# Expert results scattered to rows of the tokens, in place of a gather per choice, in a GNN and mixture-of-experts kernel

## The chip, the cores and the metric

The kernel runs on one core of a Trainium2 chip. The time is that of the device, in microseconds (us), for one execution. The engines are TensorE (PE, matmuls), VectorE (DVE), ScalarE (ACT), GpSimd (POOL) and SyncE (SP), which here only starts DMA transfers. An indirect DMA takes a list of row numbers, one for each of the 128 partitions, and moves each partition's row from such a row of a table (a gather) or to it (a scatter); in this kernel POOL issues all of them.

## The reference

Two blocks with residual connections, on 3125 nodes of 256 channels. The first is a graph attention layer over 50,000 edges; the change does not touch it. The second is a mixture of eight experts, of which each token uses the two with the largest router weights:

```python
x = x + gnn(layernorm(x), edges)
tokens = layernorm(x)
probs = softmax(tokens @ router_w.T)                # 3125 x 8
rw, re = top_k(probs, 2);  rw = rw / rw.sum(-1)     # two experts and their weights
combine = zeros(3125, 8);  combine[token, re] = rw
out = tokens
for e in range(8):
    y = gelu(tokens @ w1[e] + b1[e]) @ w2[e] + b2[e]    # 256 -> 256 -> 256
    out = out + combine[:, e:e + 1] * y
x = x + out
```

## The kernel before

The nodes are cut into 25 tiles of 128 tokens (the last has 53), one token to a partition. The graph part fills the first 790 us. Then comes the part that the change touches. It is written by hand in the order that PE, DVE, ACT and SP are to follow; POOL's order is left to the scheduler, which follows the data.

**Front.** POOL gathers the graph layer's result rows (`fetch_rows`, L1337: one gather for each token tile, 21 first and four later) into `tok_all`, 128 x 25 x 256. DVE adds a tile to `xs` (the running x) and takes its mean and variance (`add_stats`, L1377); ACT and DVE turn these into a scale (`root`, `scale`), ACT writes the normalised tokens over `tok_all` (`tokens`, L1409), PE transposes them and multiplies them with the router. The token tiles form three parts of 8, 10 and 7 (`PARTS`). For each part a `Route` finds the two experts of each token (`exps`, L1441, and on), and `places` (L1447) works out where the token goes: the (token, choice) pairs of a part are put in order of their expert, each expert's share padded to full tiles of 128 rows. `place[q]` holds the row number of a token's choice q. POOL then scatters each token row twice, by these numbers, to the table `xd` in DRAM (L1514; 16, 20 and 14 scatters). The parts make 23, 27 and 20 expert tiles, 70 in all. What of the routing isn't needed at once (the expert of each tile, the gates, part 2's places) runs as small steps inside the main loop, two to a tile.

**Main loop** (L1714), one round for each expert tile n:

- SP loads the tile n + 4 of `xd` (`load`, L1632) to `xt`.
- `turn(n + 1)` (L1647): DVE copies the expert's first weights (`w1_t`), ACT its second ones (`w2_t`), PE transposes `xt`, and DVE copies the result out (`xT`).
- `up(n)` (L1659): four matmuls, and gelu with the bias on ACT (`gT`).
- `down(n - 1)` (L1671): two matmuls, DVE copies the result to `ys`, and SP stores `ys` as 128 whole rows of the table `yd`, at the same place as the tile had in `xd`.
- ACT adds the layernormed tokens to `xs` in every second round (`with_input`).
- Two rounds after a part's last tile has been stored, POOL begins to gather its results: for each token tile and each choice one gather of 128 rows of `yd` by `place[q]` (`fetch_y`, L1685), with up to eight in flight; three rounds later DVE begins to add one of them each round, times its gate, to `xs` (`add_y`, L1692). Parts 0 and 1 make 36 gathers, of which 31 are added in the loop.

**Tail.** After the last expert tile DVE makes the adds that are left. The second bias, `combine @ b2`, is a matmul of eight rows for each token tile (`second_bias`, L1696), for which PE transposes `comb` (the gates by expert) four token tiles at a time. This runs for the 18 token tiles of parts 0 and 1, each with its store to the output (`store`, L1702); then for each of the 7 tiles of part 2 come two gathers, the bias, two adds and the store.

Of the kernel before, what the change touches and what calls it, by code (L numbers as in the profile page):

```python
# [17 lines left out]
P = 128  # L18
N = 3125
C = 256  # L20
# [40 lines left out]
def expert_tiles(a, b):  # L61

    pairs = 2 * (min(b * P, N) - a * P)
    return (pairs + EXP * (P - 1)) // P

# [326 lines left out]
def gnn_ffn_kernel(ctx: ExitStack, tc: tile.TileContext, x, src, dst, W, att_src, att_dst, bias,  # L392
# [162 lines left out]
    zrow = late.tile([P, C], F32, name="zrow")  # L555
    xd = [dram.tile([expert_tiles(a, b) * P, C], F32, name=f"xd{i}") for i, (a, b) in enumerate(PARTS)]
    yd = [dram.tile([expert_tiles(a, b) * P, C], F32, name=f"yd{i}") for i, (a, b) in enumerate(PARTS)]

    def load_late():
        for x in range(4):  # L560
            nc.sync.dma_start(b2_sb[32 * x:32 * x + EXP, :], b2)
        nc.sync.dma_start(b1_sb, b1)
        nc.sync.dma_start(rw_in, router_w)
        for i, (a, b) in enumerate(PARTS):
            nc.sync.dma_start(xd[i].rearrange("(t p) c -> p t c", p=P),
                              zrow[:, None, :].to_broadcast([P, expert_tiles(a, b), C]))
# [116 lines left out]
    G.memset(zrow, 0.0)  # L683
    nc.sync.dma_start(res[NONE:, :], bias_b[:NRES - NONE, :])
# [651 lines left out]
    tok_all = fin.tile([P, NT, C], F32, name="tok_all")  # L1336
    def fetch_rows(a, b):  # L1337
        for t in range(a, b):
            G.indirect_dma_start(out=tok_all[:, t, :], out_offset=None, in_=res,
                                 in_offset=bass.IndirectOffsetOnAxis(ap=res_row[:, t:t + 1], axis=0))  # L1340
# [15 lines left out]

    desc = fin.tile([P, EXP], F32, name="desc")
# [19 lines left out]
    def add_stats(a, b):  # L1377
        for t in range(a, b):
            V.tensor_add(xs[:, t, :], xs[:, t, :], tok_all[:, t, :])  # L1379
            V.bn_stats(st[:, t, :], xs[:, t, :])  # L1380
            V.bn_aggr(mv[:, t, :], st[:, t, :])
# [27 lines left out]
    def tokens(a, b):  # L1409

        for t in range(a, b):
            S.activation(tok_all[:, t, :], xs[:, t, :], AF.Identity, bias=c0[:, t:t + 1], scale=rs[:, t:t + 1])  # L1412
            p = psF.tile([P, 2, P], F32, name="tp")
            for kc in range(2):
                T.transpose(p[:, kc, :], tok_all[:, t, kc * P:(kc + 1) * P], ident)  # L1415
            copy_out()
            turned.append((t, p))
        if any(b == e for _, e in PARTS):
            copy_out()
            router()  # L1420
# [5 lines left out]
    class Route:  # L1426
# [20 lines left out]
        def places(self):  # L1447
# [57 lines left out]
            for q in range(2):  # L1505
                V.tensor_mul(tmp, at, oh[q])
                yield
                V.tensor_reduce(rowf, tmp, axis=AX.X, op=ALU.add)
                yield
                V.tensor_copy(place[q][:, a:b], rowf)  # L1510
# [121 lines left out]
    def load(n):  # L1632
        if n < len(tiles):
            i, j = tiles[n]
            xt[n] = fin2.tile([P, C], F32, name="xt", bufs=n_load + 2)
            nc.sync.dma_start(xt[n], xd[i][j * P:(j + 1) * P, :])
# [34 lines left out]
    def down(n):  # L1671
        if n >= 0:
# [4 lines left out]
            ys = fin2.tile([P, C], F32, name="ys", bufs=4)  # L1677
            V.tensor_copy(ys, py)  # L1678
            nc.sync.dma_start(yd[i][j * P:(j + 1) * P, :], ys)
# [5 lines left out]
    def fetch_y(i, t, q):  # L1685
        m = rows_at(t)
        y = fin2.tile([P, C], F32, name="y", bufs=8)
        G.indirect_dma_start(out=y[:m], out_offset=None, in_=yd[i],  # L1688
                             in_offset=bass.IndirectOffsetOnAxis(ap=place[q][:m, t:t + 1], axis=0))
        return t, q, y  # L1690

    def add_y(t, q, y):  # L1692
        m = rows_at(t)
        V.scalar_tensor_tensor(xs[:m, t, :], y[:m], gate[q][:m, t:t + 1], xs[:m, t, :], op0=ALU.mult, op1=ALU.add)  # L1694
# [7 lines left out]
    def store(t):  # L1702
        m = rows_at(t)
        m0 = m // 16 * 16
        nc.sync.dma_start(out[t * P:t * P + m0, :], xs[:m0, t, :])
        if m0 < m:
            nc.sync.dma_start(out[t * P + m0:t * P + m, :], xs[m0:m, t, :])

    steps = later()
    todo, fetched = {}, []  # L1710
# [3 lines left out]
    for n in range(len(tiles) + 1):  # L1714
# [5 lines left out]
        if n in ends[:-1]:  # L1720
            todo = [(i - 1, t, q) for t in range(*PARTS[i - 1]) for q in range(2)]
# [7 lines left out]
        if i and n > ends[i - 1] + 1:  # L1729
            while todo and len(fetched) < 8:  # L1730
                fetched.append(fetch_y(*todo.pop(0)))
            if n > ends[i - 1] + 4 and fetched:
                add_y(*fetched.pop(0))
    assert next(steps, 0) == 0 and not todo
    while fetched:
        add_y(*fetched.pop(0))
    cT = []
    for x in range(COMB):
        pt = psF.tile([P, P], F32, name="tp")
        T.transpose(pt, comb[:, 4 * x:4 * x + 4, :].rearrange("p t e -> p (t e)"), ident)  # L1740
        cT.append(fin.tile([P, P], F32, name=f"cT{x}"))
        S.copy(cT[x], pt)
    a, b = PARTS[-1]
    for t in range(a):
        second_bias(t)
        store(t)
    for t in (NT - 1, *range(a, NT - 1)):
        y = [fetch_y(len(PARTS) - 1, t, q) for q in range(2)]
        second_bias(t)
        for v in y:  # L1750
            add_y(*v)
        store(t)
# [29 lines left out]
```

## Time and profile before

| | us |
|---|---|
| median of 9 runs (1102.0 to 1110.7) | 1106.52 |
| the profiled execution | 1104.51 |
| its span, first to last instruction | 1102.7 |
| graph part, to | 790 |
| front: first statistics on DVE | 796.95 |
| first routing step of part 0 | 831.54 |
| main loop, first to last tile's result, about | 886 to 1075 |
| tail, last tile's copy to the end | 1074.7 to 1102.7 |

Granted clock of TensorE over the span: 0.84. Busy over the span: PE 807.0 us (73%), DVE 591.2 (54%), POOL 586.8 (53%), ACT 354.4 (32%). POOL's indirect DMAs of the changed part are 50 scatters to `xd` (50.6 us, 1013 ns each) and 50 gathers from `yd` (49.7 us, 993 ns each).

In the lines of the profile, L12 is line 12 of the kernel file, `a<-b` means that tile a is written from b, and "128x256 f32" is partitions by elements. The windows view gives the busy time and, in brackets, the number of instructions of each engine in a stretch of time; then the clock that TensorE was granted (1.00 is full speed), the share of time in which the DMA engines were busy, and the GB/s that they moved. The timeline lists instructions with their start, duration, engine and line, and the idle time of the engine before them, with the instruction or transfer that ended it; "remote" is a signal whose sender the profile could not name, and "issue" is time in which nothing that the profile shows was waited for.

### The profile page before, as it was taken

Reading aid. Unit: us, or ns where it says so; the run is one execution under the profiler, and the core shown is the slowest. Engines: PE = TensorE matmul, PEld = TensorE weight load, DVE = VectorE, ACT = ScalarE, POOL = GpSimd, SP = SyncE. Lnnn points to the kernel's source line nnn. Section 1 sums busy time; section 2 is a strip of 40 time slices with the busy share of each in tenths; the row PEclk is TensorE's granted clock in tenths of the full one; section 3 lists DMA queues with packets and bytes.
Section 4 is the critical chain, followed back from the end, with each engine's and each line's share of the span. In section 5 each row is a group of like instructions: output and inputs, shape, how many; then the busy total and the mean of one; then the engine's idle time right before and its main releaser. Section 6 shows DMA issues by size and latency. Waiting matters only on the chain. (4 is left out here: it accounts for less than half of the span.)

```text
span 1102.7 us, 14972 instructions
## 1 busy us (share of the span) xinstructions
PE 807.0 (73%) x4312; PEld 706.5 (64%) x4312; DVE 591.2 (54%) x1565; ACT 354.4 (32%) x1175; POOL 586.8 (53%) x606
## 2 busy tenths in 40 slices
PE   4842478787788787788887886899525559689794
PEld 3621377677677777677777775777324548579783
DVE  5753466557565565533444442587537315457476
ACT  3200233333333333333333332321124425356450
POOL 3857566566666666665666666304473350541335
PEclk9755689989999899989999898798855569899895
DMA  6354397444444444444444442109131223445456
GB/s 218 110 150 111 95 310 251 113 113 123 122 113 112 111 116 114 112 124 119 116 113 114 113 117 83 32 15 338 55 102 50 72 97 109 135 148 158 144 159 187
DMA packets 93883, 140.41 MB, mean 127 GB/s; under 512 B 17910, under 2 KB 72172, under 8 KB 93430
## 3 DMA queue, kind: packets, MB, share of 16 engines
q0 software_dynamic: 26640, 71.16, 24.4%
q1 hardware_dynamic: 61290, 65.48, 18.0%
q10 hardware_dynamic: 5856, 2.67, 0.9%
q8 instruction: 38, 0.62, 0.2%
q14 instruction: 59, 0.48, 0.1%
HBM read 102.74 MB, written 36.49 MB: 126 GB/s over the span
## 5 line engine op out<-in xcount | busy, mean ns | idle before, releaser
L930 POOL DMA_INDIRECT g<-xn_tab,srcS x392 | 378.0, 964 | 234.0 <-issue 92.2
L1020 PE MATMUL pz<-sel,g 128*128 128x176 f32 x1568 | 325.1, 336 | 12.4 <-issue 6.5
L1020 PEld LDWEIGHTS pz<-sel,g 128*128 128x128 f32 x1568 | 287.0, 208 | 38.7 <-issue 10.5
L1028 PE MATMUL pw<-W_sb,zs 128*128 128x256 f32 x800 | 258.9, 414 | 71.1 <-ACT zs L1022 64.4
L1022 ACT COPY zs<-pz 128x320 f32 x392 | 170.0, 434 | 409.9 <-PE pz L1020 240.7
L1028 PEld LDWEIGHTS pw<-W_sb,zs 128*128 128x128 f32 x800 | 149.4, 208 | 80.1 <-ACT zs L1022 73.3
L1514 POOL DMA_INDIRECT xd<-tok_all,place x50 | 50.6, 1013 | 88.0 <-issue 68.4
L1688 POOL DMA_INDIRECT y<-yd,place x50 | 49.7, 993 | 83.2 <-DMA yd<-ys 38.4
L1006 DVE TENSOR_TENSOR sel<-is_s,pa 128x704 f32<-128x704 f32 x100 | 82.0, 882 | 19.1 <-remote 8.6
L1665 PE MATMUL ph<-xT,w_t 128*128 128x128 f32 x560 | 79.2, 287 | 14.2 <-DVE xT L1657 11.4
L1676 PE MATMUL py<-w_t,gT 128*128 128x256 f32 x280 | 76.8, 400 | 17.2 <-issue 16.4
L1665 PEld LDWEIGHTS ph<-xT,w_t 128*128 128x128 f32 x560 | 71.7, 200 | 17.4 <-DVE xT L1657 13.9
L978 DVE COPY A<-pt 128x128 f32<-128x128 f32 x25 | 7.3, 292 | 129.1 <-PE pt L970 89.2
L1669 ACT ACTIVATE gT<-ph,bias_t 128x128 f32<-128x128 f32 x140 | 43.9, 364 | 96.6 <-PE ph L1665 57.6
L1023 ACT COPY zb<-pz 128x32 f32<-128x32 f32 x392 | 74.8, 191 | 0.2 <-DMA dr<-drel_d 0.2
L1678 DVE COPY ys<-py 128x256 f32<-128x256 f32 x70 | 29.7, 424 | 69.8 <-PE py L1676 45.1
L1676 PEld LDWEIGHTS py<-w_t,gT 128*128 128x128 f32 x280 | 50.5, 201 | 22.8 <-issue 17.4
L1041 DVE TENSOR_TENSOR ow<-pw,bias_b 128x256 f32<-128x256 f32 x22 | 9.3, 425 | 87.5 <-remote 77.0
L1415 PE MATMUL tp<-ident,tok_all 128*128 128x128 f32 x50 | 16.4, 443 | 49.2 <-ACT tok_all L1412 24.6
L999 PE MATMUL pa<-ident,A 128*128 128x128 f32 x25 | 8.5, 342 | 56.6 <-issue 23.4
L999 PEld LDWEIGHTS pa<-ident,A 128*128 128x128 f32 x25 | 3.5, 142 | 66.4 <-issue 31.5
L1652 ACT COPY w_t<-wb 128x512 f32 x70 | 43.0, 616 | 2.5 <-issue 1.7
(342 smaller groups left out, 1100.9 us busy)
## 6 DMA issues: line engine op xcount, KB each, us to landing
xt<-xd SPq DMA_DIRECT2D x70, 128.0 KB
yd<-ys SPq DMA_DIRECT2D x70, 128.0 KB
fl<-flag_d SPq DMA_DIRECT2D x50, 128.0 KB
dr<-drel_d SPq DMA_DIRECT2D x50, 128.0 KB
g<-xn_tab,srcS POOLq DMA_INDIRECT x392
xd<-zrow SPq DMA_DIRECT2D x1, 3456.0 KB
xs<-in_x_dram SPq DMA_DIRECT2D x4, 768.0 KB
out_dram<-xs SPq DMA_DIRECT2D x24, 128.0 KB
```

Of the source, the lines that this page charges most:

```text
L930: G.indirect_dma_start(out=g[-1][:, i % Q, :], out_offset=None, in_=xn_tab, in_offset=bass.IndirectOffsetOnAxis(ap=srcS[:, c:c + 1], axis=0))
L1006: V.tensor_tensor(t, is_s[:, i0:i1, None, :].to_broadcast([P, Q, H, SLOT]), pa[:, i0:i1, :, None].to_broadcast([P, Q, H, SLOT]), op=ALU.mult)
L1020: T.matmul(pz[:, kc].rearrange("p h s -> p (h s)"), g[i // Q][:, i % Q, kc * P:(kc + 1) * P], sel[i // Q][:, i % Q].rearrange("p h s -> p ...
L1022: S.copy(z[:, :, :, bass.ds(off, IC)], pz[:, :, :, :IC])
L1023: S.copy(zb[:, :, :, chunk(b, i), :].rearrange("p k h s -> p (k h) s"), pz[:, :, :, IC:].rearrange("p k h s -> p (k h) s"))
L1028: T.matmul(pw, z[:, kc, h, :P], W_sb[:, kc, h * C:(h + 1) * C], start=(i == 0 and not biased), stop=(i == CPS - 1))
L1514: ins = G.indirect_dma_start(out=xd[self.i], out_offset=bass.IndirectOffsetOnAxis(ap=place[q][:m, t:t + 1], axis=0), in_=tok_all[:m, t, :] ...
L1652: S.copy(w2_t[n], wb[:, bass.ds(expert_of(n, ACT_), 1), :])
L1665: T.matmul(ph[:, f, :], w1_t[n][:, 0, kc * C + f * P:kc * C + (f + 1) * P], xT[n][:, kc, :], start=(kc == 0), stop=(kc == 1))
L1669: S.activation(gT[n][:, f, :], ph[:, f, :], AF.Gelu, bias=routes[i].bias_t[:, f, j:j + 1])
L1676: T.matmul(py, gT[n][:, f, :], w2_t[n][:, 0, f * C:(f + 1) * C], start=(f == 0), stop=(f == 1))
L1688: G.indirect_dma_start(out=y[:m], out_offset=None, in_=yd[i], in_offset=bass.IndirectOffsetOnAxis(ap=place[q][:m, t:t + 1], axis=0))
```

## The change

The rows of `xd`, and with them `tok_all` and `xt`, become two numbers longer (`CY` = 258). The first extra column of a token's row holds the row of its first choice in `xd`, the second the address of a place of its own: each part's table `yd` gets, behind the `ROWS` rows for padding, two rows for each token. Since a token's row is scattered to both of its places, the row that an expert tile loads tells where its result is to go: if the row's own position equals the first extra number, the result is the first choice's and goes to the token's base row + 1, else to the base row; a padding row has -1 in both columns and keeps its own position. `down` works that out in two small DVE operations and POOL scatters `ys` by it, where SP stored it. Both results of a token then lie side by side, and SP loads them for a token tile with a plain DMA (`load_y`), where POOL gathered each choice.

The order of work changes too. The row numbers (`own_row`, `to_i`) are made by POOL and copied by DVE after the gathers of `fetch_rows` in the text, ahead of the first statistics. The results of part 0 are loaded and added in tiles 29 to 39, and then the second bias is added and the token tile stored in the same round; those of part 1 are loaded and added at tiles 56 to 68. In the tail the biases of the last 7 token tiles come before their loads, and those of part 1's ten come with stores on ACT's queue while the loads run. `xt` has seven buffers for six, `ys` twelve for four, `y` four for eight.

```diff
+CY = C + 2
+MOST = max(b - a for a, b in PARTS)
+ROWS = expert_tiles(0, MOST) * P
...
-    zrow = late.tile([P, C], F32, name="zrow")
-    xd = [dram.tile([expert_tiles(a, b) * P, C], F32, name=f"xd{i}") for i, (a, b) in enumerate(PARTS)]
-    yd = [dram.tile([expert_tiles(a, b) * P, C], F32, name=f"yd{i}") for i, (a, b) in enumerate(PARTS)]
+    zrow = late.tile([P, CY], F32, name="zrow")
+    xd = [dram.tile([expert_tiles(a, b) * P, CY], F32, name=f"xd{i}") for i, (a, b) in enumerate(PARTS)]
+    yd = [dram.tile([ROWS + 2 * MOST * P, C], F32, name=f"yd{i}") for i in range(len(PARTS))]
...
     G.memset(zrow, 0.0)
+    G.memset(zrow[:, C:], -1.0)
...
-    tok_all = fin.tile([P, NT, C], F32, name="tok_all")
+    tok_all = fin.tile([P, NT, CY], F32, name="tok_all")
...
+    own_row = fin.tile([P, 32], F32, name="own_row")
+    own_row_i = fin.tile([P, 32], I32, name="own_row_i")
+    G.iota(own_row_i, pattern=[[P, 32]], base=0, channel_multiplier=1)
+    to_i = fin.tile([P, NT, 1], I32, name="to_i")
+    for a, b in PARTS:
+        G.iota(to_i[:, a:b, 0], pattern=[[2 * P, b - a]], base=ROWS, channel_multiplier=2)
+    V.tensor_copy(own_row, own_row_i)
+    V.tensor_copy(tok_all[:, :, C + 1:], to_i)
     desc = fin.tile([P, EXP], F32, name="desc")
...
                 V.tensor_reduce(rowf, tmp, axis=AX.X, op=ALU.add)
                 yield
+                if not q:
+                    V.tensor_copy(tok_all[:, a:b, C:C + 1], rowf[:, :, None])
                 V.tensor_copy(place[q][:, a:b], rowf)
...
-            ys = fin2.tile([P, C], F32, name="ys", bufs=4)
+            to_f = fin2.tile([P, 1], F32, name="to_f")
+            to = fin2.tile([P, 1], I32, name="to", bufs=16)
+            V.scalar_tensor_tensor(to_f, xt[n][:, C:C + 1], own_row[:, j:j + 1], xt[n][:, C + 1:], op0=ALU.is_equal, op1=ALU.add)
+            V.tensor_max(to, to_f, own_row[:, j:j + 1])
+            ys = fin2.tile([P, C], F32, name="ys", bufs=12)
             V.tensor_copy(ys, py)
-            nc.sync.dma_start(yd[i][j * P:(j + 1) * P, :], ys)
+            ins = G.indirect_dma_start(out=yd[i], out_offset=bass.IndirectOffsetOnAxis(ap=to[:, 0:1], axis=0),
+                                       in_=ys, in_offset=None)
...
-    def fetch_y(i, t, q):
+    def load_y(i, t):
+        m, o = rows_at(t), ROWS + 2 * (t - PARTS[i][0]) * P
+        y = fin2.tile([P, 2, C], F32, name="y", bufs=4)
+        for m0, m1 in ((0, m // 16 * 16), (m // 16 * 16, m)):
+            if m0 < m1:
+                nc.sync.dma_start(y[m0:m1], yd[i][o + 2 * m0:o + 2 * m1, :].rearrange("(p s) c -> p s c", s=2))
+        return t, y
...
-        if i and n > ends[i - 1] + 1:
-            while todo and len(fetched) < 8:
-                fetched.append(fetch_y(*todo.pop(0)))
-            if n > ends[i - 1] + 4 and fetched:
-                add_y(*fetched.pop(0))
+        if i and n > ends[i - 1] + 5:
+            if todo and len(fetched) < 3:
+                fetched.append(load_y(*todo.pop(0)))
+            if n > ends[i - 1] + 8 and fetched:
+                t, y = fetched.pop(0)
+                for q in range(2):
+                    add_y(t, y, q)
+                if t < PARTS[0][1]:
+                    if t % 4 == 0:
+                        turn_comb(t // 4)
+                    second_bias(t)
+                    store(t)
...
-    for t in range(a):
-        second_bias(t)
-        store(t)
-    for t in (NT - 1, *range(a, NT - 1)):
-        y = [fetch_y(len(PARTS) - 1, t, q) for q in range(2)]
-        second_bias(t)
-        for v in y:
-            add_y(*v)
-        store(t)
+    last = [NT - 1, *range(a, NT - 1)]
+    for t in last:
+        second_bias(t)
+    fetched = [load_y(len(PARTS) - 1, t) for t in last[:4]]
+    for t in range(PARTS[0][1], a):
+        second_bias(t)
+        store(t, nc.scalar)
+    for x, t in enumerate(last):
+        y = fetched[x][1]
+        for q in range(2):
+            add_y(t, y, q)
+        store(t)
+        if x + 4 < len(last):
+            fetched.append(load_y(len(PARTS) - 1, last[x + 4]))
```

## The prediction

> **What bounds the kernel now.** I read the windows view first (columns: window, its us, busy us of PE, PEld, DVE, ACT, POOL, granted clock, DMA share, GB/s), cut at the stages that the change touches.
>
> ```profile
> 793.00:832.00 39.00, 10.79 (x49) 9.70 (x48) 14.11 (x55) 10.69 (x24) 24.77 (x26) 0.50 0.30 85
> 985.00:1032.00 47.00, 47.00 (x331) 43.09 (x330) 34.12 (x101) 31.07 (x80) 7.76 (x8) 1.00 0.51 157
> 1032.00:1049.00 17.00, 11.19 (x67) 9.93 (x67) 5.84 (x17) 5.98 (x16) 8.66 (x10) 0.80 0.47 140
> 1075.00:1103.00 28.00, 13.26 (x55) 9.16 (x55) 18.25 (x45) 1.34 (x7) 14.93 (x14) 0.56 0.61 185
> ```
>
> Until 793 nothing changes. In the expert loop PE is the bound (47.00 of 47 us, one tile per 1.98 us), except where POOL issues many indirect DMAs back to back: in 1032 to 1049 nobody is busy two thirds of the time. Why, the timeline of that place shows (start, duration, engine, line, and in brackets the idle time before and what ended it):
>
> ```profile
> 1032.06 0.95 POOL L1688 DMA_INDIRECT y<-yd,place  x1 [31.76 <-DMA yd<-ys]
> 1034.35 0.32 SPq L1679 DMA_DIRECT2D yd<-ys  x1
> 1038.62 0.63 ACT L1669 ACTIVATE gT<-ph,bias_t 128x128 f32<-128x128 f32 x2 [3.91 <-remote]
> 1041.45 0.42 DVE L1678 COPY ys<-py 128x256 f32<-128x256 f32 x1 [6.47 <-PE tp L1655]
> 1048.22 0.32 SPq L1679 DMA_DIRECT2D yd<-ys  x1
> ```
>
> From 1032.06 POOL issues eight gathers at a 1.25 us pitch, to 1041.8, and PE's signals reach ACT ("remote") and DVE about when that run ends. Between the store of tile 52 (1034.35) and of tile 55 (1048.22) lie 13.87 us where three tiles cost 5.94: 7.9 us lost. At the first run of eight (971 to 981) tiles 22 to 28 take 17.93 us instead of 11.88: 6.05 lost. Single gathers, 2 us apart (985 to 1000), cost PE nothing. The same is seen at longer runs: in the waits, ACT's gelu loses 30.7 us so, in five waits.
>
> The front (793 to 832) waits on the fetched rows and on such a stall:
>
> ```profile
> 796.95 0.43 DVE L1379 TENSOR_TENSOR xs<-xs,tok_all 128x256 f32<-128x256 f32 x1 [2.82 <-DMA tok_all<-res,res_row]
> 819.23 0.95 POOL L1339 DMA_INDIRECT tok_all<-res,res_row  x1 [0.30 <-issue]
> 820.18 0.86 POOL L1344 MEMSET comb<- 128x896 f32 x1
> 830.08 0.17 DVE L1387 RECIPROCAL ln_rs<-ln_rs 128x3 f32<-128x3 f32 x1 [17.84 <-ACT ln_rs L1384]
> 831.54 0.23 DVE L1443 TENSOR_REDUCE red<-py 128x8 f32<-128x64 f32 x1 [1.09 <-PE py L1398]
> ```
>
> DVE has the statistics of eleven tiles done by 812, then waits 17.84 us for ACT, which the gathers' run held; the first routing step starts at 831.54. Last, a steady iteration on DVE, and the tail:
>
> ```profile
> 1006.21 0.42 DVE L1678 COPY ys<-py 128x256 f32<-128x256 f32 x1 [0.49 <-PE py L1676]
> 1006.55 0.47 DVE L1694 SCALAR_TENSOR_TENSOR xs<-y,gate,xs 128x256 f32<-128x256 f32 x1
> 1006.94 0.42 DVE L1650 COPY w_t<-wa 128x512 f32 x1
> 1007.28 0.41 DVE L1657 COPY xT<-tp 128x256 f32<-128x256 f32 x1
> 1008.18 0.43 DVE L1678 COPY ys<-py 128x256 f32<-128x256 f32 x1 [0.49 <-PE py L1676]
> ...
> 1074.66 0.42 DVE L1678 COPY ys<-py 128x256 f32<-128x256 f32 x1
> 1077.45 0.42 DVE L1700 TENSOR_TENSOR xs<-xs,py 128x256 f32<-128x256 f32 x1
> 1096.47 0.95 POOL L1688 DMA_INDIRECT y<-yd,place  x1 [0.30 <-DVE xs L1694]
> 1099.52 0.48 DVE L1694 SCALAR_TENSOR_TENSOR xs<-y,gate,xs 128x256 f32<-128x256 f32 x1 [0.90 <-DMA y<-yd,place]
> ```
>
> DVE has about 0.5 us to spare per tile. After the last tile's copy (1074.66) come 28 us of biases, fourteen gathers on POOL and 24 stores.
>
> **The change, part by part.** Times are set against the profiled execution, 1104.51 (span 1102.7 and 1.8 around it), which stands 2.0 below the median.
>
> 1. *Front.* DVE works in written order, and the two new copies of row numbers stand ahead of the first statistics. The copy into tok_all needs POOL's new iotas, and in POOL's order these stand behind the 21 first gathers and the comb memset. It writes the tile that the gathers write, so it also waits for their landing. The last gather starts at 819.23 and lands some 3 us later (796.95 minus the first gather's issue gives the same); the memset ends at 821.04, and four iotas at 0.16 (the earlier iota's row) end at 821.7. So the copy starts near 822, and with it and about 1 us of constants now behind it the statistics start at 823.5, not 796.95. But before, DVE then stood 17.84 us. Now nothing is in POOL's way: eleven tiles at 0.99 us of statistics each, with ACT's chain beside them as it runs unheld, and the last tile's root, scaling, transposes and router product, about 4.5 us, bring the first routing step to about 839.2 instead of 831.54. Plus two small copies (0.2 each) on the chain: **+8**. Lower end +4.4, if ACT and PE keep fully up; upper +12, if ACT's chain of three operations per tile (tokens, copy, and stats waits) gives 1.3 us a tile.
> 2. *Two [128x1] operations per tile* before the ys copy: 0.28 together (small DVE rows), in the 0.49 us that DVE idles there: **0**. That idle is the cover; where it is used up, step 4 pays.
> 3. *70 scatters in place of 70 stores of SP and of 50 gathers, up to tile 28.* The nearest row is the xd scatter: 1.0 us busy, 1.28 pitch, under the 1.98 of a tile, so POOL keeps up; a row of 1,032 bytes instead of 1,024 costs nothing, since the edge gather moves 1,056 bytes in 0.96. In POOL's order 17 yd scatters come first, then four of part 2's xd scatters, one yd, ten xd: a run as before (14 at 945 to 964.6), lengthened by the 3 yd scatters piled up behind it: +3.5. The run of eight at 971 is gone: −6.05. Sum **−2.5**, from −6 (the backlog falls in time already lost) to +4 (the backlog loses as much as the run of eight did).
> 4. *Tiles 32 to 39.* Each now has two adds of which the second needs the first (0.40 and 0.52), and a bias add (0.42) besides the three copies and tiny operations: 2.66 us on DVE, 3.1 in the three tiles that still have routing steps. The pitch before was 1.98. Eight tiles at 0.68 or 1.1 more make **+5.5**; lower 2 (PE's own wait of 0.43 overlaps), upper 8 (the comb transposes and the bias matmul's round trip stop DVE too). On SP the y loads wait for their part's last scatter and the new stores for DVE, with the xt loads queued behind both: the first y load comes six tiles (12 us) after that scatter, and xt is fetched four tiles (8 us) ahead, so nothing is taken for it; without that cover each wait would be a load's 3 us.
> 5. *Run of eight at 1032:* gone, plain loads on SP take its place: **−7.9**. A bound from below: were half the loss something else, −4.
> 6. *Tiles 59 to 68:* two adds and the tiny operations make 2.2 us on DVE: ten times 0.2, **+1.5**, 0 to 2.5.
> 7. *Tail.* The 14 gathers on POOL, eight of the 18 bias adds and their stores have left it. What is left after the last copy: the last scatter (1.0 and about 2.5 to land), four loads that wait for it, ten bias adds beside this, then seven times two adds (0.9), store, and next load. The last store lands about 2.5 after its issue. I count 3.5 for the scatter, 3 for the load, 7 × 1.4 for the adds and loads behind four buffers, 3 for the last store: about 20, against 28.05: **−8**. Upper bound of the gain −10.5 (adds at DVE's pitch), lower −3 (3.75 MB within 13 us is near 290 GB/s, above the 185 of the window before; the front slices of the page show 338).
>
> Sum: 8 + 0 − 2.5 + 5.5 − 7.9 + 1.5 − 8 = −3.4; 1101.1 on the profile's scale, 1103 on the median's.
>
> A rule weighed on step 3. POOL's scatters run beside DVE's w_t copies. In this trace gathers beside these copies took 0.94 to 1.17 us, the longest 1.57, so the sum takes nothing for it. The Trainium skill, "SBUF — State Buffer", in its section on the bandwidth-pool intuition, has software-descriptor DMAs slowed five times by DVE copies running beside them. By that, an estimate, a scatter would take 4.9 us, POOL would pace the tiles, and the sum would be +200 us. The row is of this chip and this kind of overlap, so it decides; no run here has had a scatter beside every tile.
>
> **The rivals.**
> - *The loops on DVE cost more* (steps 4 and 6 at 2 + 8 more): the bias goes DVE→PE→DVE in written order behind DVE's adds, with PE's matmuls for the next tile queued behind it. For: DVE idles only 0.5 per tile. Against: PE has the bias matmul's input long before. About 1112.
> - *Slower: the scatters count as one run.* A scatter every 1.98 us for 70 tiles might hold PE's signals as eight at 1.25 us do (6 to 8 us per eight). It decides if the threshold lies between a pitch of 1.25 and 2 us; 985 to 1000 (2 us apart, no loss) speaks against it, with only eight in a row. At 3 of 9 groups hit, +25: near 1130.
> - *Faster by more:* front at +4.4 and tail at −10.5, scatter backlog without cost: sum about −12, near 1094.
> - *The tail doesn't get shorter:* the loads still queue behind the last scatter and stores crowd the DMAs; step 7 at 0 and all else as counted: about 1111, or 1108 with a third of the gain.
>
> **How the numbers follow.** This kernel can tell about 0.3% (3.3 us) from no change. Forecast (−3.4, ±4): 0.42, of it 0.22 below 1103.2, 0.15 within 0.3%, 0.05 above. DVE loops 0.22, slower. One run 0.10, slower. Faster by more 0.18. Tail 0.08, of it 0.05 within, 0.03 slower. So faster 0.40, same 0.20, slower 0.40. The range goes from the front's and tail's best ends together (−15: 1091) to the sum with the upper ends of steps 1, 3 and 4 (+4, +6.5, +2.5 on −3.4: 1116), and little above it for the first rival: 1119; the one-run rival stays out. The likeliest case alone: 1099 to 1107.
>
> **What would show it.** Right: DVE's first statistics add (L1379 before) near 823 and the first routing reduce near 839; no run of eight after 970 and no eight-microsecond hole near 1032; a tile pitch of 1.98 where scatters alone are added and 2.6 to 3 in tiles 32 to 39; some 20 us from the last ys copy to the end. Wrong: "remote" waits through the whole loop, POOL scatters starting later and later against their ys copies, or a front whose statistics start at 797 as now.

## The result and the profile after

The changed kernel takes 1116.89 us (median of 15 runs, 1113.77 to 1123.1) against 1105.74 before (46 runs, 1099.01 to 1110.7): a ratio of 1.0108, 95% interval 1.0092 to 1.0125. It is 1.1% slower. The forecast was 1103, in a range of 1091 to 1119; 1116.89 lies inside the range, but on the other side of no change.

The profiled execution took 1124.35 us, 7.5 above its median. Its graph part, which the change leaves alone, ended 8 us later than in the profile before (the first row gather starts at 802.14 here and at 793.97 before), so I count from that gather on. From there to the end it is 320.3 us, against 308.8 before: 11.5 more, which is what the medians say too.

Stage by stage, from the timelines (starts of the first row gather, of the first routing reduce, and of DVE's copies of the tiles' results to ys; tile 0 is the first, copied at 906.06 before; the 886 given above for the loop's start is its first matmul), in us. The first row is a part of the second, so the sum leaves it out:

| stage | before | after | difference | forecast |
|---|---|---|---|---|
| first gather to first routing reduce | 37.6 | 47.3 | +9.8 | +8 |
| first gather to tile 0 | 112.1 | 122.0 | +9.9 | +8 |
| tiles 0 to 17 | 39.7 | 40.0 | +0.3 | 0 |
| tiles 17 to 31 | 46.5 | 50.3 | +3.8 | −2.5 |
| tiles 31 to 39 | 15.9 | 24.1 | +8.2 | +5.5 |
| tiles 39 to 58 | 45.5 | 38.0 | −7.5 | −7.9 |
| tiles 58 to 69 | 21.0 | 24.9 | +4.0 | +1.5 |
| tile 69 to the end | 28.1 | 20.9 | −7.1 | −8 |
| sum | 308.8 | 320.3 | +11.5 | −3.4 |

The windows view of the changed kernel, cut at these stages (window, its us, busy us of PE, PEld, DVE, ACT, POOL, granted clock, DMA share, GB/s):

```profile
802.00:849.50 47.50, 10.27 (x48) 9.48 (x48) 13.29 (x55) 9.88 (x24) 25.09 (x30) 0.50 0.24 69
...
964.00:989.00 25.00, 10.04 (x54) 8.23 (x53) 5.78 (x24) 3.58 (x10) 17.84 (x17) 0.70 0.35 110
1014.40:1038.60 24.20, 22.93 (x134) 16.93 (x133) 22.02 (x71) 12.07 (x31) 9.11 (x9) 1.00 0.60 181
1064.70:1070.60 5.90, 5.90 (x44) 5.44 (x43) 4.10 (x15) 4.22 (x12) 2.92 (x3) 1.00 0.75 217
1076.60:1101.50 24.90, 22.78 (x144) 18.93 (x142) 23.80 (x71) 12.12 (x32) 9.84 (x11) 1.00 0.51 158
1101.50:1122.50 21.00, 7.57 (x40) 5.18 (x37) 13.00 (x32) 1.14 (x5) 1.83 (x2) 0.63 0.61 195
```

In 1064.7 to 1070.6 (tiles 52 to 55) PE is busy throughout: the hole of the eight gathers is gone. In 964 to 989 it is busy 10 of 25 us: a larger hole than any before (13.9 of 22 us at the run of fourteen, 945 to 967), and the granted clock goes down with it, from 1.00 until 973 to 0.50 at 982 to 989. And in two stretches DVE is nearly full: 22.0 of 24.2 us (tiles 31 to 39, where PE is fuller still, 22.9) and 23.8 of 24.9 (tiles 58 to 69).

The timeline of the changed kernel, at the front, in the large hole, in a round with adds, and in the tail:

```profile
802.14 0.98 POOL L1346 DMA_INDIRECT tok_all<-res,res_row  x1 [11.03 <-DVE rwT L1356]
...
829.65 0.19 DVE L1371 CAST tok_all<-to_i 128x25 f32<-128x25 int32 x1 [0.28 <-POOL to_i L1369]
830.64 0.42 DVE L1394 TENSOR_TENSOR xs<-xs,tok_all 128x256 f32<-128x256 f32 x1
849.49 0.23 DVE L1458 TENSOR_REDUCE red<-py 128x8 f32<-128x64 f32 x1 [1.33 <-PE py L1413]
...
962.87 0.97 POOL L1701 DMA_INDIRECT yd<-ys,to  x1 [0.90 <-DVE rowf L1523]
964.15 0.42 DVE L1700 COPY ys<-py 128x256 f32<-128x256 f32 x1
966.14 1.06 PE L1682 MATMUL ph<-xT,w_t 128*128 128x128 f32 x8
969.61 1.16 PE L1682 MATMUL ph<-xT,w_t 128*128 128x128 f32 x8 [1.33 <-DVE xT L1674]
973.05 0.63 ACT L1686 ACTIVATE gT<-ph,bias_t 128x128 f32<-128x128 f32 x2 [6.14 <-remote]
977.34 0.42 DVE L1700 COPY ys<-py 128x256 f32<-128x256 f32 x1 [7.46 <-remote]
982.03 2.07 PE L1682 MATMUL ph<-xT,w_t 128*128 128x128 f32 x8 [6.58 <-issue]
985.89 0.98 POOL L1701 DMA_INDIRECT yd<-ys,to  x1 [0.31 <-issue]
988.03 0.63 ACT L1686 ACTIVATE gT<-ph,bias_t 128x128 f32<-128x128 f32 x2 [13.85 <-remote]
988.71 0.42 DVE L1700 COPY ys<-py 128x256 f32<-128x256 f32 x1 [6.42 <-remote]
...
1084.71 0.97 POOL L1701 DMA_INDIRECT yd<-ys,to  x1 [1.49 <-DVE ys L1700]
1085.27 0.65 DVE L1667 COPY w_t<-wa 128x512 f32 x1
...
1101.54 0.42 DVE L1700 COPY ys<-py 128x256 f32<-128x256 f32 x1
1105.12 2.08 SPq L1716 DMA_DIRECT2D y<-yd  x5
1110.73 3.73 DVE L1721 SCALAR_TENSOR_TENSOR xs<-y,gate,xs 53x256 f32<-53x256 f32 x8
```

From 962.87 to 985.9 POOL issues eighteen indirect DMAs at a pitch of 1.28 us, 1.87 for the last two of part 2 (a scatter of ys, fourteen of part 2's rows with one of ys among them, two more of ys). From tile 17 (964.15) to tile 20 (988.71) three tiles take 24.6 us. The eight matmuls at 982.03, at the lower clock, take 2.07 us where they took 1.06. For comparison the run of fourteen in the kernel before, with the results of tiles 17 (948.13) and 22 (968.16):

```profile
945.27 0.97 POOL L1514 DMA_INDIRECT xd<-tok_all,place  x1 [42.45 <-issue]
948.13 0.42 DVE L1678 COPY ys<-py 128x256 f32<-128x256 f32 x1 [0.92 <-PE tp L1655]
957.01 0.63 ACT L1669 ACTIVATE gT<-ph,bias_t 128x128 f32<-128x128 f32 x2 [5.42 <-remote]
963.00 1.56 POOL L1514 DMA_INDIRECT xd<-tok_all,place  x1 [0.30 <-issue]
968.16 0.42 DVE L1678 COPY ys<-py 128x256 f32<-128x256 f32 x1 [0.98 <-PE py L1676]
```

In the waits of the changed kernel (us in all, number of waits, the longest) the late signals are:

```profile
ACT gT L1686 <- remote: 39.6, 5, 13.9
DVE ys L1700 <- remote: 28.0, 3, 14.1
```

Of ACT's 39.6 us, 20.0 stand at the run of eighteen; of the 30.7 before, 5.4 stood at the run of fourteen and 7.9 at the second run of eight. The rest, in both kernels, stands beside the run of twenty scatters ahead of the first tile or just behind it, which the change leaves as it was.

### The profile page after: what moved, and what is told of

Its sections match the earlier page's. It is cut to its first block, busy times and chain, and to the rows that moved or that the text cites. A ratio compares the mean times of both kernels' runs of the same rounds, so it can differ in the third digit from the quotient of the medians.

```text
span 1122.5 us, 15036 instructions
## 1 busy us (share of the span) xinstructions
PE 814.0 (73%) x4312; PEld 709.9 (63%) x4312; DVE 614.0 (55%) x1710; ACT 354.8 (32%) x1175; POOL 605.0 (54%) x631
## 3 DMA queue, kind: packets, MB, share of 16 engines
q0 software_dynamic: 27216, 73.98, 24.1%
## 5 line engine op out<-in xcount | busy, mean ns | idle before, releaser
L1035 PE MATMUL pw<-W_sb,zs 128*128 128x256 f32 x800 | 261.9, 418 | 80.2 <-ACT zs L1029 75.5
L1027 PEld LDWEIGHTS pz<-sel,g 128*128 128x128 f32 x1568 | 290.1, 210 | 35.0 <-ACT zb L1030 8.8
L1701 POOL DMA_INDIRECT yd<-ys,to x70 | 69.0, 986 | 94.4 <-DVE ys L1700 47.8
L1682 PE MATMUL ph<-xT,w_t 128*128 128x128 f32 x560 | 79.6, 287 | 15.8 <-DVE xT L1674 7.9
L1013 DVE TENSOR_TENSOR sel<-is_s,pa 128x704 f32<-128x704 f32 x100 | 82.0, 882 | 15.8 <-remote 7.8
L1693 PE MATMUL py<-w_t,gT 128*128 128x256 f32 x280 | 77.1, 401 | 15.9 <-issue 15.9
L1700 DVE COPY ys<-py 128x256 f32<-128x256 f32 x70 | 29.7, 425 | 48.3 <-remote 28.0
L1430 PEld LDWEIGHTS tp<-ident,tok_all 128*128 128x128 f32 x50 | 9.3, 244 | 62.4 <-issue 35.1
```

The source lines that it names most:

```text
L1013: V.tensor_tensor(t, is_s[:, i0:i1, None, :].to_broadcast([P, Q, H, SLOT]), pa[:, i0:i1, :, None].to_broadcast([P, Q, H, SLOT]), op=ALU.mult)
L1027: T.matmul(pz[:, kc].rearrange("p h s -> p (h s)"), g[i // Q][:, i % Q, kc * P:(kc + 1) * P], sel[i // Q][:, i % Q].rearrange("p h s -> p ...
L1035: T.matmul(pw, z[:, kc, h, :P], W_sb[:, kc, h * C:(h + 1) * C], start=(i == 0 and not biased), stop=(i == CPS - 1))
L1682: T.matmul(ph[:, f, :], w1_t[n][:, 0, kc * C + f * P:kc * C + (f + 1) * P], xT[n][:, kc, :], start=(kc == 0), stop=(kc == 1))
L1693: T.matmul(py, gT[n][:, f, :], w2_t[n][:, 0, f * C:(f + 1) * C], start=(f == 0), stop=(f == 1))
L1701: ins = G.indirect_dma_start(out=yd[i], out_offset=bass.IndirectOffsetOnAxis(ap=to[:, 0:1], axis=0), in_=ys, in_offset=None)
```

## The experiments

Each ratio is to the kernel before, timed on the same chip: e1 to e8 on one (the kernel before takes 1094 us there), e9 and e10 on another (1101). The stages are from one profiled execution of each, in us as in the table above (front: first gather to first routing reduce; total: first gather to the end, with the stage from the routing to tile 0 that the columns leave out); a dash stands where one time alone was taken. The profiles before and after were taken earlier, with the 46 and 15 runs above. The stage from the first routing reduce to tile 0 takes 74.5 and 74.7 us in the profiles before and after, but 71.7 to 72.6 in all of e1 to e8 (71.0 and 68.6 in e9 and e10), whether they have the change or not. So for e1 to e8 2 to 3 us of a total's distance to the first two rows come from a stage that the runs weren't meant to touch; between them it falls away.

| run | front | 0-17 | 17-31 | 31-39 | 39-58 | 58-69 | tail | total | ratio (95%) |
|---|---|---|---|---|---|---|---|---|---|
| before | 37.6 | 39.7 | 46.5 | 15.9 | 45.5 | 21.0 | 28.1 | 308.8 | 1 |
| after | 47.3 | 40.0 | 50.3 | 24.1 | 38.0 | 24.9 | 20.9 | 320.3 | 1.0108 (1.0092 to 1.0125) |
| e1_front | 37.2 | 40.3 | 50.3 | 23.9 | 38.1 | 25.3 | 21.4 | 309.0 | 1.0033 (1.0006 to 1.0060) |
| e2_bias | 47.2 | 39.8 | 49.9 | 20.3 | 38.0 | 24.9 | 26.0 | 317.9 | 1.0143 (1.0113 to 1.0173) |
| e3_spaced | 47.2 | 40.5 | 35.4 | 23.8 | 46.4 | 24.9 | 22.2 | 312.7 | 1.0081 (1.0049 to 1.0113) |
| e4_oneadd | 46.7 | 40.8 | 47.9 | 16.2 | 37.7 | 24.9 | 26.4 | 313.0 | 1.0103 (1.0064 to 1.0143) |
| e5_all | 37.2 | 40.4 | 33.9 | 18.3 | 48.3 | 22.0 | 20.7 | 292.6 | 0.9916 (0.9886 to 0.9946) |
| e6_addsfirst | 47.2 | 40.7 | 50.9 | 22.6 | 38.4 | 22.3 | 22.2 | 316.8 | – |
| e7_beforespaced | 37.2 | 40.2 | 31.9 | 15.9 | 37.8 | 20.4 | 32.3 | 288.1 | 0.9843 (0.9804 to 0.9881) |
| e8_groups | 47.1 | 39.4 | 36.7 | 28.7 | 39.8 | 24.9 | 21.3 | 310.7 | – |
| e9_fold | 38.9 | 41.2 | 37.6 | 18.7 | 43.3 | 22.4 | 18.0 | 291.1 | 0.9845 (0.9793 to 0.9897) |
| e10_beforefold | 37.1 | 41.2 | 32.6 | 15.8 | 37.7 | 21.4 | 29.7 | 284.0 | 0.9810 (0.9765 to 0.9854) |

Theory: the slowdown is three things on top of the gains that were forecast, namely the front's statistics behind a copy, a longer run of back-to-back indirect DMAs, and rounds in which DVE has more than a tile's time (1.98 us) to do. Rivals: the front's shift is absorbed later; another cause sits at the places of the holes; the bias matmul, not DVE, slows tiles 32 to 39.

### The front

```diff
-    V.tensor_copy(own_row, own_row_i)
-    V.tensor_copy(tok_all[:, :, C + 1:], to_i)
...
                 if not q:
+                    if not self.i:
+                        V.tensor_copy(own_row, own_row_i)
+                    V.tensor_copy(tok_all[:, a:b, C + 1:], to_i[:, a:b])
                     V.tensor_copy(tok_all[:, a:b, C:C + 1], rowf[:, :, None])
```

> The two DVE copies of row numbers (own_row, and the base rows in tok_all) are taken from ahead of the first statistics and made in `places`, each part's own columns beside its first-choice copy. If the front's loss is that DVE's statistics wait behind the copy for all gathers: first statistics 3 us after the first gather's issue (now 28.5), first routing reduce 37.6 to 38.5 us after it (now 47.35), and about 9.5 us less in all, near 1107. If the delay only moves stalls from one place to another, the first routing reduce is still earlier, but the time of the first tile's result is not, and the total stays at 1113 to 1117.

The timeline of that run:

```profile
785.10 0.98 POOL L1346 DMA_INDIRECT tok_all<-res,res_row  x1 [11.26 <-DVE goes_on L1387]
...
788.23 0.42 DVE L1392 TENSOR_TENSOR xs<-xs,tok_all 128x256 f32<-128x256 f32 x1 [2.99 <-DMA tok_all<-res,res_row]
...
820.85 0.17 DVE L1400 RECIPROCAL ln_rs<-ln_rs 128x3 f32<-128x3 f32 x1 [17.58 <-ACT ln_rs L1397]
822.31 0.23 DVE L1456 TENSOR_REDUCE red<-py 128x8 f32<-128x64 f32 x1 [1.09 <-PE py L1411]
```

The statistics start 3.1 us after the gather, the routing 37.2 us after it, and DVE's old wait of 17.6 us is back. Every later stage is as in the changed kernel, so the shift was not absorbed anywhere: 11.3 us less from the first gather to the end, namely 10.1 in the front and 2.2 in the stage that is shorter in every profile of e1 to e8, with 1 us the other way over the rest. By the ratios it is 1.0033 instead of 1.0108, 0.75% or 8 us, which the intervals of the two allow.

### The bias and the adds

Part 0's bias, comb transposes and stores were moved from the loop to the tail:

```diff
-                if t < PARTS[0][1]:
-                    if t % 4 == 0:
-                        turn_comb(t // 4)
-                    second_bias(t)
-                    store(t)
...
-    for t in range(PARTS[0][1], a):
+    for t in range(a):
         second_bias(t)
         store(t, nc.scalar)
```

> The second bias, the comb transposes and the stores of part 0's eight token tiles are taken out of the loop and made in the tail, with part 1's. If DVE's own work paces tiles 32 to 39, tiles 31 to 39 take about 18 us (now 24.1; DVE 2.2 to 2.3 a tile is left) and the tail grows by at most 8 x 0.42 = 3.4: 1111 to 1114. If the bias matmul's round trip over PE was the brake, tiles 31 to 39 take 15.9 us as before the change, and the total is near 1110. If the tail takes all that the loop gains, 1117.

Tiles 31 to 39 took 20.3 us, not 18, and the tail grew by 5.1, not by 3.4. What the loop gained (3.8) the tail took, and more, so the rival of the tail was the nearest and the ratio is no better than the changed kernel's. Two adds in a round were left, and with them the rounds take 2.46 us or more (one to 2.66): DVE works nearly without a pause there, and in five of eight its w_t copy takes 0.63 or 0.64 us instead of 0.42 (see "A DVE copy beside a scatter"). But the rival of the bias matmul is not refuted: in the changed kernel these matmuls start 2.75 or 2.76 us apart in five of seven intervals, which is PE's row with a bias, as a later run shows. Either work alone, two adds or a bias, is more than 1.98 us; together PE is the slower by a little.

With, in addition, one add in a round:

```diff
-                t, y = fetched.pop(0)
-                for q in range(2):
-                    add_y(t, y, q)
+                if i == 1:
+                    t, y = fetched[0]
+                    add_y(t, y, half)
+                    half = 1 - half
+                    if not half:
+                        fetched.pop(0)
```

> As the run that takes part 0's biases, comb transposes and stores to the tail, and also only one add of part 0 in a round (rounds 32 to 47). By DVE's sum (1.7 us a tile) tiles 31 to 47 go at PE's 1.98, 31.7 us for sixteen, against about 18 + 16 with two adds in a round: 2 us less than that run, 1109 to 1112. If two adds in a row weren't the brake, the same time as that run.

Tiles 31 to 39 took 16.2 us and 39 to 47 15.8: PE's pace in all sixteen, as DVE's sum said. Against the run with two adds and no bias (20.3 and 16.1), 4.4 us less, where 2 were expected, since two adds had cost more than I had counted. By the ratios (1.0103 and 1.0143) the gain is 0.4%, with intervals that overlap.

### The long run of indirect DMAs

Part 2's scatters were held back, one to every second round, by a copy of their row numbers in that round:

```diff
+        def scatter(self, t, q):
+            m, at = P if t < NT - 1 else LAST, place[q][:, t:t + 1]
+            if self.i == 2:
+                at = fin2.tile([P, 1], I32, name="at_row", bufs=4)
+                V.tensor_copy(at, place[q][:, t:t + 1])
...
         for _ in range(2):
             next(steps, None)
+        if n % 2 == 0 and getattr(routes[2], "held", None):
+            routes[2].scatter(*routes[2].held.pop(0))
```

> Part 2's 14 scatters to xd are no longer issued at once: one in every second round of the loop, each held back by a small DVE copy of its row numbers in that round. Nothing else is changed. If long unbroken runs of POOL's indirect DMAs hold PE's signals, no hole of many us is left in tiles 17 to 31, which then take 28 to 31 us (now 50.3): near 1097. If POOL's load as such does it (three DMAs of 1.28 us in the 3.96 us of two tiles is nearly unbroken), the holes spread over tiles 18 to 45 and the total is 1117 or more. If the holes are made by something else in tiles 17 to 31, they stay where they are.

Tiles 17 to 20 took 7.9 us instead of 24.6, and 17 to 31 35.4 instead of 50.3: the hole goes with the run, though not all the way to 31. A new wait took 8.3 us of the 14.9 back, at tiles 47 to 52 (18.2 us, 9.9 in the changed kernel). The timeline there:

```profile
1006.77 24.36 SPq L1659 DMA_DIRECT2D xt<-xd  x12
...
1020.69 1.56 POOL L1538 DMA_INDIRECT xd<-tok_all,at_row  x1 [0.30 <-DVE xT L1680]
...
1030.19 0.42 DVE L1680 COPY xT<-tp 128x256 f32<-128x256 f32 x1 [5.15 <-PE tp L1678]
```

The last of the fourteen scatters starts at 1020.69, and the first tile of part 2 cannot be loaded before it has landed; PE waits 6.1 us for that load, and DVE for PE. One scatter in two rounds from round 18 on is simply too late for tile 50. In the next kernels part 2's places are worked out first (the two generators in `later()` swapped), so that they start at round 10.

How long may a run be? The same kernel with the places first and groups of four:

```diff
+        for _ in range(4):
+            if n % 8 == 0 and getattr(routes[2], "held", None):
+                routes[2].scatter(*routes[2].held.pop(0))
```

> The changed kernel with part 2's places first and its xd scatters in groups of four, in rounds 16, 24, 32 and 40, so that with the ys scatters that pile up behind them runs of six or seven form. If a hold needs some eight DMAs in a row, tiles 17 to 31 take 30 to 33 us, as with single ones; if the loss is in proportion to the DMAs of a run (18.6 us for 17, so 1.1 each), each group costs 6 to 7 us: 42 us for tiles 17 to 31.

Runs of seven formed (four and the ys scatters behind them), three times. Tiles 17 to 31 took 36.7 us, 1.3 more than with single ones (2.8 more than in the run with all mends, where the places come first too) and 5 less than in proportion; by the profile's naming no late signal of over 1 us stands beside these three runs, and one of 4.0 us behind a run of eight later on. So a run of seven doesn't make the holds that fourteen and eighteen make, but it is not free: tiles 31 to 39, where the third run fell, took 28.7 us instead of 24.1. Single scatters are not free either: PE's pace for tiles 17 to 31 is 27.7 us, and 35.4 were taken with them.

The same test on the kernel before, which has no scatter of ys at all:

```diff
+            if self.i == 2:
+                at = fin2.tile([P, 1], I32, name="at_row", bufs=4)
+                V.tensor_copy(at, place[q][:, t:t + 1])
...
-        y = fin2.tile([P, C], F32, name="y", bufs=8)
+        name, bufs = ("y", 3) if i < 2 else ("y_last", 8)
+        y = fin2.tile([P, C], F32, name=name, bufs=bufs)
...
-            while todo and len(fetched) < 8:
+            while todo and len(fetched) < 3:
...
+        if getattr(routes[2], "held", None):
+            routes[2].scatter(*routes[2].held.pop(0))
```

> The kernel before the change, with its POOL transfers spread: part 2's 14 xd scatters one to a round from round 10, and the y gathers of parts 0 and 1 with three buffers instead of eight, so that no run of eight forms. If runs of back-to-back indirect DMAs are what costs tiles 17 to 28 and 52 to 55 their time, tiles 17 to 31 take 28 to 31 us (46.5 before) and 52 to 55 5.9 (13.9): 23 to 26 us less, a ratio near 0.978. If another cause sits at these places, the holes stay.

The holes of 12.5 and 8 us went: 31.9 us for tiles 17 to 31 and 6.2 for 52 to 55. Of the 4.2 us left over PE's pace (27.7), 3.5 stand in tiles 22 to 28, where seven scatters and gathers still came together. Its windows view, over tiles 17 to 31 and 52 to 55:

```profile
933.00:965.00 32.00, 29.61 (x203) 26.24 (x201) 22.13 (x85) 18.39 (x48) 16.74 (x16) 1.00 0.56 168
1006.60:1012.90 6.30, 6.30 (x46) 5.69 (x44) 3.77 (x11) 4.13 (x11) 2.40 (x3) 1.00 0.68 191
```

POOL is busy half of the first stretch, with 16 instructions, and PE 29.6 of 32 us. The ratio is 0.9843 (0.9804 to 0.9881), a smaller gain than the forecast 0.978; the tail grew by 4.3 us; the smaller number of y buffers, for which its left-over gathers now wait, is the likely reason, not a shown one. So the kernel before gains 1.6% by spreading its transfers alone. That is more than the change with all its mends reached without the fold (0.9916, 0.9886 to 0.9946, the next section but one, on the same chip).

### A DVE copy beside a scatter

In eight of the rounds 59 to 68 of the changed kernel the w_t copy takes 0.64 to 0.65 us where it takes 0.42 in most others; it starts 0.55 us after a scatter started, as in the pair of lines shown above (1084.71 and 1085.27). The adds, with the bias and the load, were put ahead of the ys copy:

```diff
         up(n)
-        down(n - 1)
         i = tiles[min(n, len(tiles) - 1)][0]
...
                     second_bias(t)
                     store(t)
+        down(n - 1)
```

> In each round the y load, the adds, and part 0's bias and store stand ahead of the row number operations, the ys copy and the scatter, instead of behind them. The work is the same. If the w_t copy is slow (0.64 for 0.42 us) in rounds 59 to 68 because it starts 0.55 us after a scatter starts, it now starts before the scatter does, takes 0.42, and tiles 58 to 69 take 22.5 to 23 us instead of 24.9. If DVE's sum alone set the pace, tiles 58 to 69 stay at 24.9.

Tiles 58 to 69 took 22.3 us instead of 24.9. The copy now starts ahead of the scatter:

```profile
1075.41 0.42 DVE L1667 COPY w_t<-wa 128x512 f32 x1
...
1075.77 0.97 POOL L1701 DMA_INDIRECT yd<-ys,to  x1 [1.34 <-DVE ys L1700]
```

The order alone was worth 2.7 of the 4.0 us that this stage had lost: a round takes 2.25 us now and took 2.46, in both DVE works without a pause, and the 0.22 between them is the copy. Eight slow copies make 1.8 of the 2.7; the 1.3 that stay are DVE's sum.

Over all twelve profiles the pattern is sharper than "slower". Of 127 w_t copies that started more than 0.50 us after a scatter's start and more than 0.21 us before its end, 125 ended 0.22 to 0.24 us after that scatter's end; of 270 that started earlier in a scatter or gather, none took more than 0.45 us. DVE's other copies, adds and small operations were not longer there.

### All mends together, and the bias folded in

> All the mends together: the row number copies moved into `places`; part 2's places worked out first in the loop and its xd scatters one in every second round from round 10; one add of part 0 in a round (rounds 32 to 47), its biases and stores in rounds 48 to 55; part 1's adds from round 56, one or two in a round. By the stages of the runs before: front 37.5 us after the first gather, tiles 17 to 31 about 30 us (50.3 in the changed kernel), 31 to 39 16, 39 to 58 38 to 39, 58 to 69 23 to 25, tail 21: 284 to 288 us from the first gather to the end, against 308.8 before the change and 320.3 after it, so a ratio of 0.977 to 0.981 to before. If the holes come back elsewhere (as in the run with spaced scatters, where tiles 47 to 52 took 18.2 us), 295 and a ratio of 0.988.

The total from the first gather on is 292.6 us, 6.6 above the forecast's middle, and the ratio 0.9916, not 0.977 to 0.981: tiles 39 to 58 took 48.3 us. These are the rounds that carry the bias now (48 to 55), at 2.75 us a round without any add of y. The timeline of PE in one such round:

```profile
1009.71 1.03 PE L1700 MATMUL py<-w_t,gT 128*128 128x256 f32 x4
...
1010.67 0.69 PE L1741 MATMUL py<-b_sb,cT 8*128 8x256 f32 x2
...
1011.29 0.44 PE L1679 MATMUL tp<-ident,xt 128*128 128x128 f32 x2
...
1011.57 1.06 PE L1689 MATMUL ph<-xT,w_t 128*128 128x128 f32 x8
...
1012.46 1.03 PE L1700 MATMUL py<-w_t,gT 128*128 128x256 f32 x4
```

PE has no gap: the bias matmul (0.69) stands in its row beside 1.03, 0.44 and 1.06, and the round is 2.75 us (1009.71 to 1012.46) instead of 1.98. PE bounds these rounds, and for a bias in the loop I had counted no PE time at all. The same holds for the changed kernel's tiles 31 to 39, with a bias and two adds: there too PE's row is 2.75 us from one bias matmul to the next, and PE is busy 10.64 of 11.0 us from 1025 to 1036, DVE 9.92.

The bias can be had without PE: DVE adds the expert's row of b2 while it copies the result out of PSUM.

```diff
-            V.tensor_copy(ys, py)
+            V.tensor_add(ys[:, None, :], py[:, None, :], b2_all[:, bass.ds(owner[n], 1), :])
```

> The kernel with all the mends, and the second bias folded into the copy of an expert tile's result: DVE adds the expert's row of b2 (kept on all partitions) while it takes the result from PSUM, so the comb tile, its transposes and 25 bias matmuls and adds fall away. In the run with all mends a round with a bias took 2.75 us where 1.98 is PE's pace, and the bias adds stand ahead of the last adds in the tail. If PE's bias matmul is what those rounds pay for: tiles 39 to 58 37.7 us (48.3 in the run with all mends), tail 17 to 18 (20.7): 276 to 281 us from the first gather to the end, a ratio near 0.975. If these rounds are slow for the store on SP or for the single adds, tiles 39 to 58 stay above 45.

Tiles 47 to 55 went back to 16.2 us (23.1 in the run with all mends) and the tail to 18.0, but tiles 39 to 58 took 43.3 and 17 to 31 37.6: the total is 291.1, not 276 to 281. Single rounds of 3 to 4.7 us were left, in the stretch in which part 2's scatters run among those of ys. In one of them:

```profile
1002.59 1.56 POOL L1539 DMA_INDIRECT xd<-tok_all,at_row  x1 [0.30 <-DVE to_f L1700]
1003.18 1.20 DVE L1670 COPY w_t<-wa 128x512 f32 x1
```

The copy takes 1.20 us instead of 0.42 and ends 0.23 after the scatter. The scatter's 1.56 is its own: the two scatters of the last token tile take 1.55 us or more in every profile, in the kernel before too (963.00, shown above, with no such copy beside it). That accounts for a part of it; over all rounds the w_t copies are 3.8 us longer than at 0.42 each. What else is slow in those rounds I have not settled.

> The same fold in the kernel before the change with its POOL transfers spread (gathers kept). Tiles 0 to 69 as in that run (about 146 us); the tail keeps 14 gathers of 1.28 us on POOL and the left-over adds but loses 25 biases, 28 us (32.3 there). If the change's own worth is its tail alone, this run is 8 to 12 us behind the changed kernel with the same mends: 283 to 287 us from the first gather to the end. If scatters cost more in the loop than they save in the tail, it is level with it or ahead.

The same fold with gathers ended at 284.0 us, as early as its forecast had it, but 7 us ahead of the scatter version and not 8 to 12 behind it. Tiles 17 to 58 took 86.1 us here and 99.6 with scatters; the tail took 29.7 and 18.0; a further 4.1 us of the 7 stand ahead of tile 0. By the ratios the two are level (0.9810, 0.9765 to 0.9854, and 0.9845, 0.9793 to 0.9897). So with the same mends, what scattering saves in the tail (11.7 us) it spends in the loop (13.5), where POOL has 84 transfers instead of 50. Both are faster than the two kernels that this text set out from.

## Why the prediction was wrong, point by point

- **Step 1, front (+8; measured +9.8 at the routing, +9.9 at tile 0).** Right in mechanism and place: the statistics start 28.5 us after the first gather (29.5 by the forecast's times), and taking the copies away gives 10 us back. The chain of statistics and ACT took 18.9 us for what I had put at 15.7.
- **Step 2 (0; measured +0.3 over tiles 0 to 17).** Right. The two small operations and the scatter of ys cost nothing where POOL isn't crowded.
- **Step 3, the run of part 2's scatters (−2.5; measured +3.8).** This is the step that failed most: 6.3 us of the 14.9 between forecast and measurement. With the 2.7 of step 4 and the 2.5 of step 6 it makes up the whole 11.5 us of the loss. I had "lengthened by the 3 yd scatters piled up behind it: +3.5", that is, their POOL time. Tiles 17 to 22 became 8.2 us longer (22.4 before, 30.6 after). A run doesn't cost its own length beyond PE's work, it holds PE's signals: fourteen cost 12.5 us over PE's pace in these five tiles, eighteen 20.7. Part of that is the granted clock, which fell to 0.50 in the longer hole. The gain at the run of eight was 4.6, not 6.05, because tiles 25 to 28 stay at 7.4 us in the changed kernel.
- **Step 4, tiles 32 to 39 (+5.5; measured +8.2).** The step has a slip of its own: five tiles at 0.68 more and three at 1.1 make 6.7, not 5.5. DVE's sum was a limit by itself, as forecast (two adds and no bias: 2.46 us and more; one add and no bias: PE's pace). But PE's 0.69 us for a bias matmul was in no term, and it lifts PE's own round to 2.75, above DVE's 2.66; eight such rounds are 22.0 of the 24.1 us. The rival "the loops on DVE cost more" named the bias's round trip, and what the runs showed is plain PE time.
- **Step 5 (−7.9; measured −7.5)** and **step 7 (−8; measured −7.1)**: right in place and size. The 338 GB/s that step 7 calls "the front slices" is of a slice at 744 to 772 us, in the graph part; nothing in the forecast of −8 rests on it.
- **Step 6, tiles 59 to 68 (+1.5; measured +4.0).** DVE's work was 2.2 us by my sum and 2.47 in fact; 0.22 of the difference, in eight rounds, is the w_t copy beside a scatter. Here the rule that I had weighed and put at nothing deserves its due. The Trainium skill, "SBUF — State Buffer", in its section on the bandwidth-pool intuition, describes a lock between POOL's descriptor writing and DVE's copies, with the DMA as the loser. The scatters themselves lost little (0.986 us on average for 70, not five times more), as forecast; the loser was mostly DVE's copy, 0.42 to 0.65, held until 0.23 us after the scatter's end. The row that I had weighed against the rule was only about POOL's side.
- **The rivals.** The time came out near the rival with costlier loops (1112) plus the hold of the run. The rival of an unshortened tail failed (−7.1), and so did "faster by more" (the front cost 9.8, not 4.4). The one-run rival, signals held through the whole loop, did not occur: with a scatter every 1.98 us PE is busy 5.90 of 5.90 us in tiles 52 to 55.

All four misses are on the same side. Each upper end was in the text (+12, +4, +8, +2.5); their sum with steps 2, 5 and 7 is +10.6, close to the +11.5 that came, but two of the four went past their ends (8.2 and 4.0) while the front stayed below its own. That 1116.89 falls inside the range owes something to luck. I had taken the nearest row for each and never the thought that each row was taken with an engine that had time to spare.

## What to carry to other kernels

Count the longest unbroken run of POOL's indirect DMAs before and after a change, not their number: in these runs two runs of seven cost 1.3 to 2.8 us together over single scatters and a third 4.6, eight gathers 6 to 8, fourteen scatters 12.5 and eighteen 21, and spreading them made the kernel before 1.6% faster without touching its work. Length alone doesn't set the price: nine in a row in the run with all mends (987 to 1000) cost about 2 us over PE's pace in tiles 39 to 47. The runs of 16 and 20 scatters ahead of the first tile stand in every kernel here, with late signals of up to 14 us beside them, and no run spread them. When work moves into a loop, add it up for every engine of that loop, for PE too, and look for instructions that will now run beside others. A wait that is written ahead of a stage costs nothing only if that stage's first operand isn't there yet.

## What the runs showed of the hardware

- During long runs of indirect DMAs PE's results reach ACT and DVE late: in the changed kernel PE was done with a tile's first matmuls at 967.2 and ACT began on them at 973.05; with the next at 970.8, and ACT began at 988.03, just after the run had ended (986.9). Why is open. The runs show the condition (long and dense runs; at one scatter in 1.98 us PE was busy 5.90 of 5.90 us), not the mechanism.
- DVE's 128x512 copy takes 0.42 us, but if it starts later than 0.50 us into a scatter it ends 0.22 to 0.24 us after the scatter does (125 of 127 copies): 0.64 to 0.65 us at the 0.55 that is most frequent, and 1.18 and 1.20 beside the two scatters of 1.56. In the kernel before no copy was longer than 0.46, but only one started at such a point. Whether gathers do the same is not shown: in no run did a copy start at such a point of a gather.
- The granted clock was 1.00 where PE worked without a hole and fell to 0.50 within the hole at the run of eighteen (982 to 989), where eight matmuls took 2.07 us instead of 1.06.
- Left open, too: in e1 to e5 the kernels with the change are, by their ratios, 3 to 7 us slower against the kernel before than their stages from the first gather on say (e1_front: 1.0033, though its stages sum to the same 309 us), and the kernel before with its transfers spread is so by 3.5. Two to three us of this are the stage from the routing to tile 0, which was shorter in every profile of e1 to e8. The rest could lie in the graph part or in the spread of single profiled executions; no run separates the two.
